# Moving expert steps out of the last attention unit, and the second half's norm into the gap behind it

## The chip, the cores and the metric

The kernel runs on one core of one Trainium2 chip. The metric is the device time of the program in microseconds, as the median of several runs. The profile is of one further execution. Its engines are TensorE (PE, with PEld for the loading of weights), VectorE (DVE), ScalarE (ACT) and GpSimd (POOL), and SyncE's queue (SP), which issues most DMAs. [...]

## The reference, cut to what matters

Tokens `x` (1024 of 128 features) pass through four layers. Each layer adds a cross-attention to a context of 6404 rows and then a mixture of experts, both on the layer-normed tokens:

```
x = x + _L1_xattn_ref(_layernorm(x), ctx, ctx, ...)
x = x + _L1_ffn_ref(_layernorm(x), ...)      # 8 experts, top 1
x = x + _L2_xattn_ref(...)                   # softmax over the heads
x = x + _L2_ffn_ref(...)                     # fake-quantised, gated
x = x + _L3_xattn_ref(...)
x = x + _L3_ffn_ref(_layernorm(x), ...)      # 8 experts, top 2
```

Attention of layers 1 and 3 has 16 heads of 8 features and a softmax over the context. An expert of layer 1 is `gelu(x w1 + b1) w2 + b2`, with `w1` of 128 x 512 and `w2` of 512 x 128; the token's best expert is added. An expert of layer 3 also adds its input, and the sum is normalised over its features, scaled by `gamma`, shifted by `beta`, and weighted by the softmax over the two best. All experts are computed for all tokens, and the weights of those not chosen are zero.

## The kernel before

The tokens are cut into two halves of 512. `attn_softmax` does attention for layers 1 and 3 in 16 units, a pair of heads and a half each; the last unit is the last pair with the second half. A unit goes over the 51 blocks of 128 keys in 26 steps. A step makes scores (L1133, `x_ps` and `y_ps`), exponentials (L1138, ACT), and the products with the values of the step before (L1023, `o_ps`). Between them, at each `M` of the step's written order, goes other work: in all units but the last the maxima of the next unit (`more_max`).

In the last unit there are no maxima left. There two generators run instead. `also` is the experts for the first half of the tokens (`ffn1` in layer 1, `ffn3` in layer 3), whose tokens are complete when the unit before is finished; `beside`, in layer 1 alone, makes the keys of layer 2 (`heads_keys`). Every step has two `M`, each of which takes one step of `beside` and, from step 9 on, one of `also`:

```
for what in order[i % 3]:
    if what == "M":
        more_max()
        next(beside, None)
        if u == UNITS - 1 and i >= 9:
            next(also, None)
```

The steps of `also` are: `normed` (layer norm on DVE with its power on POOL at L114, then, five steps on, four transposes on PE at L142 and a copy to `xnT` on DVE at L156), the router, and for each of eight experts (`expert`) twice a pair of steps. The first of a pair issues two hidden blocks (L1195 on PE, Gelu at L1196 on ACT); the second runs what waits, the second matmuls (L1184) of the part before and, after an expert's second part, the weighted add to the tokens. That is `add_weighted` in layer 1 (L624) and `add_normed` in layer 3 (L1752 to L1766: sum, statistics, a power on POOL, scaling, add). An expert's start also issues loads of its weights on SP (L1172, L1173), and in layer 3 of `gamma` and `b2` to `gb` (L1771, L1772) with two buffers, from which POOL makes `xb` (L1774).

When the unit's last values are multiplied, `finish` sets four things into the table `later`: `out_of_banks` at once (a copy by ACT and two DMAs through memory that bring the sums of the softmax to `dr`), then `inverted` (L1045, DVE, and two DMAs to `rr`), `normalized` (L1055 on PE with `rr`, L1056 on DVE), `projected` (L1062 on PE, L1066 adds to the tokens on DVE) and an empty one. Behind the last unit they are run one after the other, with five steps of `also` ahead of each, and after them whatever is left of `beside` and `also`.

PE, ACT and DVE follow the order as written in this part (`tc.manual_schedule`); POOL and SP are put in order by the framework's scheduler, from its own costs, and so is all that is outside such a part. After attention of layer 1 follow the set-up of attention of layer 2 (`attn_heads`: queries for the first half, first maxima), then the experts for the second half (`experts_apart`, which is `ffn1(1, ...)`), then the quantisation of the weights of the layer 2 network. After attention of layer 3 follow only the experts for the second half (`ffn3(1, ...)`) and the store of the output.

Of the kernel before, what the change touches and what calls it, by code (L numbers as in the profile page):

```python
# [35 lines left out]
def done(steps):  # L36

    while True:
        try:
            next(steps)  # L40
        except StopIteration as end:
            return end.value


class Net:
# [3 lines left out]
    def __init__(self, ctx, tc, a, out):  # L49
        self.tc, self.nc, self.a, self.out = tc, tc.nc, a, out  # L50
        nc = self.nc
        self.const = ctx.enter_context(tc.tile_pool(name="const", bufs=1))
        self.small = ctx.enter_context(tc.tile_pool(name="small", bufs=3))
        self.xp = ctx.enter_context(tc.tile_pool(name="xp", bufs=2))
        self.ps_h = self.ps_m = self.ps_pair = None
        self.ident = self.const.tile([P, P], F32, name="ident")
        make_identity(nc, self.ident)
        self.identb = self.const.tile([P, P], BF16, name="identb")
        nc.vector.tensor_copy(self.identb, self.ident)
        self.ones = self.const.tile([P, P], F32, name="ones")  # L60
        nc.vector.memset(self.ones, 1.0)
        self.nhalf = self.const.tile([P, NT], F32, name="nhalf")
        nc.vector.memset(self.nhalf, -0.5)
        self.cols = self.const.tile([P, a["cols"].shape[1]], F32, name="cols")
        nc.sync.dma_start(out=self.cols, in_=a["cols"])
        self.x = self.const.tile([P, NT, D], F32, name="x")
        nc.sync.dma_start(out=self.x, in_=a["x"].rearrange("(t p) d -> p t d", p=P))
# [79 lines left out]
    def normed(self, half):  # L147

        nc = self.nc
        xn = self.xp.tile([P, HT, D], F32, tag="xn", name="xn")  # L150
        xnT = self.xp.tile([P, HALF], F32, tag="xnT", name="xnT")
        self.layernorm(xn, self.tokens(half), HT)
        for _ in range(4):
            yield
        m = self.transposed(xn, HT)
        nc.vector.tensor_copy(xnT, m)  # L156
        yield
        return xn, xnT

    def tokens(self, half):  # L160
        return self.x[:, HT * half : HT * half + HT]
# [562 lines left out]
    def attn_softmax(self, ctxT, L, bo, before, last, keys_early=False):  # L724
# [18 lines left out]
        UNITS = 2 * PAIRS  # L743
# [5 lines left out]
        with ExitStack() as st:  # L749
# [256 lines left out]
            def more_max():  # L1006
                u, i = divmod(made[0], per_unit)
                if u >= UNITS:
                    return
                max_group(u, i)  # L1010
                made[0] += 1
                if i == per_unit - 1:
                    max_found(u)
                    later.setdefault(step + 2, []).append(lambda: max_to_rows(u))
# [4 lines left out]
            def values(u, i, o, pts):  # L1019
                for (c, g), pt in pts.items():  # L1020
                    h = units[u][0] + PAIRS * g
                    j = 2 * (c % 2) + g
                    nc.tensor.matmul(  # L1023
                        o[32 * j : 32 * j + 32], v[:, c, ds(VW * h, 32)], pt,
                        start=i == 0, stop=c + 2 >= NK,
                    )
# [76 lines left out]
            also = beside = iter(())  # L1103
            for u in range(UNITS):
                p = units[u][0]
                if u == UNITS - 1:
                    pairs.close()
                    self.bank_pools(tail, f"a{L}t", h=2, m=2)
                    also, beside = last(tail, kb, kS[(PAIRS - 2) % 2])
                accs[u] = None  # L1110
                pending = [(c, g) for c in range(NK) for g in range(2)]
                place = {}
                for i, cs in enumerate(pairs_of_keys):
                    for what in order[i % 3]:
                        if what == "M":
                            more_max()
                            next(beside, None)
                            if u == UNITS - 1 and i >= 9:
                                next(also, None)
                        elif what == "S":  # L1120
                            two = (len(place) % 3) == 0
                            some = [pending.pop(0) for _ in range(min(len(pending), 2 if two else 1))]
                            if not some:
                                continue
                            if two:
                                s = ps_x.tile([P, 2, HALF], F32, tag="x", name="x_ps")
                                pt = pr.tile([P, 2, HALF], F32, tag="px", name="px", bufs=3)
                            else:
                                s = ps_y.tile([P, 1, HALF], F32, tag="y", name="y_ps")
                                pt = pr.tile([P, 1, HALF], F32, tag="py", name="py", bufs=3)  # L1130
                            for k, (c, g) in enumerate(some):
                                r = slice(64 * g, 64 * g + KR)
                                nc.tensor.matmul(  # L1133
                                    s[:, k], kS[p % 2][r, ts(c, P)], qS[u % 2][r],
                                    start=True, stop=True,
                                )
                                place[c, g] = pt[:, k]
                            nc.scalar.activation(pt[:, : len(some)], s[:, : len(some)], AF.Exp)  # L1138
                        elif waiting:
                            uu, ii, pts = waiting.pop(0)  # L1140
                            if accs[uu] is None:
                                accs[uu] = ps_o.tile([P, HALF], F32, tag="o", name="o_ps")
                            values(uu, ii, accs[uu], pts)
                            if ii == STEPS - 1:
                                finish(uu, accs[uu], step)
                    waiting.append((u, i, {(c, g): place[c, g] for c in cs for g in range(2)}))
                    if made[0] < per_unit + ahead + (step + 1) * per_unit / STEPS:
                        more_max()
                    for f in later.pop(step, ()):
                        f()  # L1150
                    step += 1
# [1 line left out]
            values(uu, ii, accs[uu], pts)  # L1153
            finish(uu, accs[uu], step)
            for at in sorted(later):
                for _ in range(5):
                    next(also, None)
                for f in later[at]:
                    f()
            done(beside)  # L1160
            done(also)


# [42 lines left out]
    def ffn1(self, half, pool, w_tile, hidden_tile):  # L1206
        nc, a = self.nc, self.a
        E = 8
        wr = pool.tile([P, E], F32, name="wr")
        br = pool.tile([P, E], F32, name="br")  # L1210
        b2 = pool.tile([E, D], F32, name="b2")
        nc.sync.dma_start(out=wr, in_=a["L1_ffn_wr"])
        nc.sync.dma_start(out=br, in_=a["L1_ffn_br"].partition_broadcast(P))
        nc.sync.dma_start(out=b2, in_=a["L1_ffn_b2"])
        xn, xnT = yield from self.normed(half)
        sc = pool.tile([P, HT, E], F32, name="sc")
        nc.vector.tensor_tensor(
            sc, self.router(xnT, wr, E), br.unsqueeze(1).to_broadcast([P, HT, E]), ALU.add
        )
        cw = self.ranks_below(pool, sc, E, 1)  # L1220
        waiting = []

        def bias():
            self.add_projected(self.weights_transposed(pool, cw, E), b2, half)

        for e in range(E):
            got = yield from self.expert(1, e, xnT, w_tile, hidden_tile, waiting)
            waiting.append(lambda got=got, e=e: self.add_weighted(got["y"], half, cw, e))
            if e == 0:
                waiting.append(bias)  # L1230
        while waiting:
            waiting.pop(0)()
            yield
# [496 lines left out]
    def ffn3(self, half, pool, w_tile, hidden_tile):  # L1730
# [3 lines left out]
        beta = pool.tile([E, D], F32, name="beta")  # L1734
        nc.sync.dma_start(out=wr, in_=a["L3_ffn_router_w"])
        nc.sync.dma_start(out=beta, in_=a["L3_ffn_beta"])
        xn, xnT = yield from self.normed(half)
        lg = pool.tile([P, HT, E], F32, name="lg")
        nc.vector.tensor_copy(lg, self.router(xnT, wr, E))
        sel = self.ranks_below(pool, lg, E, 2)  # L1740
# [27 lines left out]
        for e in range(E):  # L1768
# [6 lines left out]
            got = yield from self.expert(3, e, xnT, w_tile, hidden_tile, waiting)  # L1775
# [231 lines left out]
```

## Time and profile before

| | us |
|---|---|
| median of 3 runs | 7865.02 |
| lowest and highest | 7858.43 and 7870.11 |
| the profiled execution | 7869.13 |
| its span in the profile | 7867.4 |

In the profiled execution, from the timeline:

| | layer 1 | layer 3 |
|---|---|---|
| last `o_ps` product of the unit starts | 4043.43 | 7760.00 |
| `inverted` starts on DVE (L1045) | 4052.38 | 7775.54 |
| selector matmul on PE (L1055) | 4055.93 | 7778.82 |
| projection on PE (L1062) | 4058.13 | 7781.69 |
| router of the second half's experts on PE (L575) | 4080.29 | 7789.58 |
| last second matmul of the second half's experts starts | 4139.79 | 7847.03 |

Times in the timeline are microseconds from the span's start. A row has the start, the duration, the engine, the line of the kernel, the operation with its output and inputs, and in brackets how long the engine stood idle before it and what released it. In the rows of windows, the column PEclk is the clock that was granted to PE, as a share of the full one. Granted over the whole span: 0.966.

### The profile page before, as it was taken

The numbers are of one execution on the slowest core, as the hardware profiler recorded it, in microseconds if no ns is written. First come the engines' busy times: TensorE is split into PE (matmuls) and PEld (weight loads), VectorE is DVE, ScalarE is ACT, GpSimd is POOL, SyncE is SP. The second block draws the span as 40 slices with busy tenths as digits, with TensorE's granted clock in tenths as the row PEclk, the third lists the DMA queues.
The fourth block names the chain that finished last, engine by engine and source line by source line (L and its number), as shares of the span: only waits on it lengthen the run. The fifth ranks groups of instructions, "written<-read, shape, count | busy, mean of one in ns | idle before, by whom it ended". The sixth has DMA issues, their size and how long they took to land.

```text
span 7867.4 us, 105018 instructions
## 1 busy us (share of the span) xinstructions
PE 7290.1 (93%) x41897; PEld 2775.1 (35%) x42105; DVE 5689.6 (72%) x6628; ACT 4999.0 (64%) x6063; POOL 2594.5 (33%) x1460
## 2 busy tenths in 40 slices
PE   6999999999999889999997999998899978999997
PEld 2333333333333433333343333333333333333334
DVE  6555555555553388888737999989999988888854
ACT  2444444444444457777766888877788856777765
POOL 4999989989999610000010000000000010000001
PEclk8999999999999889999998999999999988999988
DMA  1000000000000201001030000000000011101001
GB/s 30 1 2 1 2 2 1 2 2 1 1 1 1 77 24 17 15 11 20 25 122 14 14 14 13 14 11 11 12 14 13 14 51 27 19 12 20 12 6 40
DMA packets 144769, 134.94 MB, mean 17 GB/s; under 512 B 30954, under 2 KB 125478, under 8 KB 143310
## 3 DMA queue, kind: packets, MB, share of 16 engines
q1 hardware_dynamic: 134022, 105.19, 6.0%
q0 software_dynamic: 5296, 17.22, 0.7%
q8 instruction: 330, 5.41, 0.3%
q10 hardware_dynamic: 4960, 5.80, 0.2%
q14 instruction: 161, 1.32, 0.1%
HBM read 105.46 MB, written 35.85 MB: 18 GB/s over the span
## 4 chain that ended last, share of the span: by engine, by line
PE 73%; DVE 15%; ACT 5%; POOL 3%; issue 2%; DMA 1%; SPq 0%; ACTq 0%; POOLq 0%; DVEq 0%
PE o_ps L348 10%; PE x_ps L326 9%; PE s_ps L1479 8%; PE o_ps L1023 8%; DVE mx L909 8%; PE o_ps L1535 5%; PE x_ps L1133 5%; PE x_ps L1467 5%; ACT px L1138 3%; PE b_ps L281 3%; PE pair_ps L1367 3%; PE y_ps L1133 2%; PE x_ps L1463 2%; POOL acc L342 2%; PE x_ps L316 2%
## 5 line engine op out<-in xcount | busy, mean ns | idle before, releaser
L342 POOL TENSOR_TENSOR acc<-acc,pt 128x1024 f32<-128x1024 f32 x912 | 2150.0, 2357 | 116.2 <-ACT pt L331 63.0
L909 DVE TENSOR_REDUCE mx<-pair_ps 128x2 f32<-128x1024 f32 x1612 | 1811.1, 1177 | 245.9 <-PE pair_ps L905 225.9
L285 DVE TENSOR_REDUCE mx<-b_ps 128x2 f32<-128x1024 f32 x920 | 1095.0, 1190 | 1059.5 <-PE b_ps L281 1059.2
L331 ACT ACTIVATE pt<-x_ps,bias 128x1024 f32<-128x1024 f32 (+1 forms) x944 | 1003.7, 1110 | 817.8 <-PE x_ps L326 715.3
L1138 ACT ACTIVATE px<-x_ps 128x1024 f32<-128x1024 f32 x1088 | 1113.7, 1024 | 315.3 <-PE x_ps L1133 307.1
L1527 DVE TENSOR_TENSOR e<-e,inv 128x1024 f32<-128x1024 f32 (+1 forms) x816 | 993.5, 1219 | 10.7 <-DVE inv L1520 0.5
L348 PE MATMUL o_ps<-pt,v 128*64 128x512 f32 (+1 forms) x3776 | 916.0, 605 | 0.0
L1023 PE MATMUL o_ps<-px,v 128*32 128x512 f32 x4352 | 906.8, 621 | 0.0
L1023 PE MATMUL o_ps<-py,v 128*32 128x512 f32 x2176 | 899.4, 619 | 0.0
L326 PE MATMUL x_ps<-q,kT 64*128 64x512 f32 (+1 forms) x3776 | 893.5, 592 | 0.0
L1376 ACT CAST lb<-pair_ps 128x1024 bf16<-128x1024 f32 (+1 forms) x714 | 720.3, 1009 | 264.2 <-PE pair_ps L1367 239.4
L905 PE MATMUL pair_ps<-kb,qz 64*128 64x512 bf16 (+1 forms) x3224 | 823.8, 385 | 55.5 <-DVE mx L909 38.3
L1470 ACT ACTIVATE e<-x_ps 128x1024 f32<-128x1024 f32 (+1 forms) x816 | 840.5, 1030 | 24.7 <-PE x_ps L1467 22.9
L1138 ACT ACTIVATE py<-y_ps 128x512 f32<-128x512 f32 x1088 | 647.6, 595 | 325.2 <-PE y_ps L1133 321.4
L1479 PE MATMUL s_ps<-e,ident 128*128 128x512 f32 (+1 forms) x1632 | 848.4, 602 | 0.4
L1133 PE MATMUL x_ps<-qS,kS 33*128 33x512 f32 x2176 | 713.6, 533 | 126.2 <-ACT px L1138 126.1
L1133 PE MATMUL y_ps<-qS,kS 33*128 33x512 f32 x1088 | 569.2, 523 | 7.3 <-ACT py L1138 7.3
L897 POOL TENSOR_SCALAR qz<-qbf,cols 128x512 bf16<-128x512 bf16 x31 | 48.7, 1572 | 1557.0 <-PE y_ps L1133 1505.9
L1535 PE MATMUL o_ps<-e,vz 128*32 128x256 f32 (+1 forms) x6528 | 535.6, 398 | 7.6 <-DVE e L1527 7.4
L1421 POOL MEMSET kS<- 128x512 f32 x2 | 1.1, 526 | 1591.7 <-PE x_ps L1463 1591.7
L1384 DVE TENSOR_TENSOR low<-lb,low 128x1024 bf16<-128x1024 bf16 (+1 forms) x714 | 488.0, 683 | 14.3 <-ACT lb L1376 14.2
L1467 PE MATMUL x_ps<-mneg,identb 128*128 128x512 bf16 x1424 | 453.0, 388 | 40.4 <-issue 33.0
(378 smaller groups left out, 8475.6 us busy)
## 6 DMA issues: line engine op xcount, KB each, us to landing
kS<-kst SPq DMA_DIRECT2D x400, 64.0 KB
kS<-kd SPq DMA_DIRECT2D x120, 200.1 KB
w<-in_L_ffn_w SPq DMA_DIRECT2D x48, 256.0 KB
kst<-kd POOLq DMA_DIRECT2D x24, 512.0 KB, 13.4
kd<-kh SPq DMA_DIRECT2D x12, 512.0 KB
kd<-k SPq DMA_DIRECT2D x12, 512.0 KB
qS<-qd SPq DMA_DIRECT2D x256, 16.0 KB
kb<-in_L_ffn_w SPq DMA_DIRECT2D x16, 256.0 KB
```

The lines of the kernel that those rows point to most:

```text
L285: nc.vector.tensor_reduce(mxs[u][:, t, :, b], m[:, :, :n], AX.X, ALU.max)
L326: nc.tensor.matmul(s[:n, g], kT[p % 2][r, at : at + n], qs[p][r, ts(half, HALF)], start=False, stop=True,)
L331: nc.scalar.activation(pt[:n], s[:n], AF.Exp, bias=bias[:n, c : c + 1])
L342: nc.gpsimd.tensor_tensor(accs[u][:n], first[:n], pt[:n], ALU.add)
L348: nc.tensor.matmul(o[cols], v[:n, c, cols], pt[:n, g], start=c == 0, stop=c == NKT - 1)
L909: nc.vector.tensor_reduce(mxs[u][:, t, b], m[:, :, :n], AX.X, ALU.max)
L1023: nc.tensor.matmul(o[32 * j : 32 * j + 32], v[:, c, ds(VW * h, 32)], pt, start=i == 0, stop=c + 2 >= NK,)
L1133: nc.tensor.matmul(s[:, k], kS[p % 2][r, ts(c, P)], qS[u % 2][r], start=True, stop=True,)
L1138: nc.scalar.activation(pt[:, : len(some)], s[:, : len(some)], AF.Exp)
L1479: nc.tensor.matmul(firsts[i], self.ident[:n], es[i, h // 4][:n, h % 4], start=k == 0, stop=k == K - 1,)
L1527: nc.vector.tensor_tensor(e, e, r, ALU.mult)
L1535: nc.tensor.matmul(outs[half][32 * g : 32 * g + 32, cols], vz[i % 2][:n, ds(P * j + 32 * g, 32)], es[i, j][:n, g, cols], start=c == 0 and ...
```

## The change

In the last unit of layers 1 and 3, `also` is stepped at two of three steps only, the steps whose number is not a multiple of 3. Behind the unit, two of its steps go ahead of each of the four functions in `later`, instead of five. Then, with `beside` finished, the layer norm and the transposes of the second half of the tokens are issued here, with one step of `also` after each of the norm's own steps, and the result is kept in `self.ready`. The rest of `also` follows. When the experts of the second half start, they take the kept result instead of computing it (`normed_or_ready`).

```
-        self.ps_h = self.ps_m = self.ps_pair = None
+        self.ps_h = self.ps_m = self.ps_pair = self.ready = None
...
+    def normed_or_ready(self, half):
+
+        if half and self.ready:
+            got, self.ready = self.ready, None
+            return got
+        return (yield from self.normed(half))
...
-                            if u == UNITS - 1 and i >= 9:
+                            if u == UNITS - 1 and i >= 9 and i % 3:
                                 next(also, None)
...
             for at in sorted(later):
-                for _ in range(5):
+                for _ in range(2):
                     next(also, None)
                 for f in later[at]:
                     f()
             done(beside)
+
+            other = self.normed(1)
+            while True:
+                try:
+                    next(other)
+                except StopIteration as end:
+                    self.ready = end.value
+                    break
+                next(also, None)
             done(also)
...
-        xn, xnT = yield from self.normed(half)
+        xn, xnT = yield from self.normed_or_ready(half)
```

The last pair of lines stands twice, in `ffn1` and in `ffn3`.

## The prediction

> **What bounds the kernel now.** I read the page first, then the last unit of layers 1 and 3 by windows, then the chain and the timeline there. The page:
>
> ```profile
> span 7867.4 us, 105018 instructions
> PE 7290.1 (93%) x41897; PEld 2775.1 (35%) x42105; DVE 5689.6 (72%) x6628; ACT 4999.0 (64%) x6063; POOL 2594.5 (33%) x1460
> PE 73%; DVE 15%; ACT 5%; POOL 3%; issue 2%; DMA 1%; SPq 0%; ACTq 0%; POOLq 0%; DVEq 0%
> ```
>
> TensorE (PE) bounds the whole, so a gain must come from places where PE stands still. The windows of layer 3's end (start:end, length, busy PE, PEld, DVE, ACT, POOL, granted clock, DMA share, GB/s) show where:
>
> ```profile
> core 0: us, PE busy (x) PEld busy (x) DVE busy (x) ACT busy (x) POOL busy (x), PEclk, DMA share, GB/s
> 7616.00:7624.00 8.00, 7.24 (x28) 1.69 (x24) 0.00 (x0) 4.05 (x5) 0.00 (x0) 0.50 0.01 3
> 7712.00:7720.00 8.00, 8.00 (x48) 4.92 (x47) 4.66 (x17) 7.67 (x9) 1.18 (x2) 1.00 0.20 66
> 7768.00:7776.00 8.00, 0.00 (x0) 0.00 (x0) 6.38 (x21) 0.00 (x0) 1.01 (x1) 0.65 0.00 0
> 7776.00:7784.00 8.00, 4.12 (x10) 2.28 (x10) 0.88 (x2) 0.00 (x0) 0.00 (x0) 0.50 0.02 2
> 7784.00:7792.00 8.00, 3.67 (x13) 2.94 (x14) 4.17 (x19) 0.00 (x0) 3.49 (x3) 0.50 0.01 2
> ```
>
> PE is full while experts and attention share a step (second row), does nothing for 8 us after the unit (third), and limps until 7792. The timeline says why, and what a step with an expert part holds:
>
> ```profile
> 7714.22 1.98 PE L1195 MATMUL h_ps<-xnT,w 128*128 128x512 f32 x4
> 7717.97 2.05 PE L1184 MATMUL m_ps<-w,kb 128*128 128x128 f32 x16
> 7718.00 1.28 ACT L1138 ACT_TABLE_LOAD   x1
> ...
> 7769.06 0.68 DVE L1752 TENSOR_TENSOR res<-m_ps,xb 128x512 f32<-128x512 f32 x1
> 7775.54 0.16 DVE L1045 TENSOR_TENSOR dr<-dr 128x8 f32<-128x8 f32 x1
> 7778.82 2.04 PE L1055 MATMUL m_ps<-rr,selr 2*128 2x512 f32 x2 [10.94 <-DMA rr<-rd]
> 7787.55 1.25 PE L142 MATMUL m_ps<-ident,xn 128*128 128x128 f32 x4 [3.77 <-DVE xn L133]
> ```
>
> The softmax inverse (L1045) stands on DVE behind the last expert's normed add (from L1752), and PE waits 10.94 us for its round trip; then 3.77 us for the second half's norm. Layer 1 has the same tail (4.63 and 4.49 us), with cheap adds (1.13 us). Last, the chain of waits gives a step without expert work (the eight `o_ps` matmuls of each step):
>
> ```profile
> 3897.08 0.99 PE o_ps L1023 x8
> 3898.75 0.99 PE o_ps L1023 x8
> 3901.36 0.99 PE o_ps L1023 x8
> 3905.05 1.00 PE o_ps L1023 x8
> 3906.47 1.87 PE o_ps L1023 x8
> ```
>
> Four steps in 9.39 us: 2.35 us each.
>
> **The change: the loop.** `also` has 40 resumptions: 1 to 5 norm and transposes, an expert part (`h` and Gelu) at 6, 8, ... 36, and the second matmuls at the odd ones between. Before, steps 9 to 25 make 34: 15 parts in the loop, one behind it. Now eleven steps make 22: 9 parts in the loop, 7 behind it. Six parts leave the loop in each layer, with twelve ACT table loads (1.28 us each) that lie beside PE work. A step with a part takes 6.11 us in layer 3 (`h_ps` starts from 7702.32 to 7751.23, eight intervals), 6.17 in layer 1. Layer 1: 6 x 6.17 - 6 x 2.35 = 22.9 us shorter. In layer 3 the bare steps before the first part run at clock 0.50, 3.88 us each (`o_ps` from 7607.85 to 7631.13, six steps); two of the six are there: 36.7 - 2 x 3.88 - 4 x 2.35 = 19.5 us shorter.
>
> **The tail of layer 1.** From the loop's last `o_ps` (4043.96) to the projection's end (4060.21) is 16.3 us before. After, I lay PE's work end to end at 1.8 us for each `h` group or second group (4045.74 to 4047.73 in the tail of before, less its wait): four groups to 7.2; the inverse needs 0.7 (copy) + 3.8 (7610.43 to 7614.22, where nothing held it) + 0.4 + 3.1 (4052.87 to 4055.93) = 8.0, so PE waits 0.8; selector matmul 1.05; two groups; projection 1.1; six groups; transposes 0.7; four groups: end at 32.5. That is 16.2 later against 22.9 earlier: -6.7. The norm's DVE work (1.7 + 1.1 us) and POOL power (1.0) lie beside the six groups; without that cover they cost the 4.5 us they cost before.
>
> Behind it, attention of layer 2 starts. Its POOL queue held both halves' powers ahead of an all-reduce on which DVE waited 5.8 us; one power less is -1.0. The second half's expert could also start earlier than 4080.3, since its tokens are ready: between 0 and -4 (the idle PE there); I take -1. From there experts, quantisation and attention follow rigidly. Layer 1: -8.7.
>
> **The tail of layer 3.** Here an add takes some 6.1 us of DVE and POOL (7857.02 to 7863.11), and every add's `xb` needs a `gb` load which starts when the add before the last has let go:
>
> ```profile
> 7840.80 0.33 SPq L1771 DMA_DIRECT2D gb<-in_L_ffn_gamma  x1
> 7844.22 1.27 POOL L1774 TENSOR_TENSOR xb<-xn,gb 128x512 f32<-128x512 f32 x1 [5.56 <-DMA gb<-in_L_ffn_b]
> 7845.44 1.02 POOL L114 TENSOR_TENSOR rstd<-ve,nhalf 128x4 f32<-128x4 f32 x1
> ```
>
> The power stands behind that `xb` on POOL, so adds come every 7.9 us. Five now lie in the tail. In DVE's order: add 3 ends at 8.1 after the loop, the inverse behind it gives `rr` at 11.6, PE (done at 7.2) waits 4.4 us, falls to half clock and does the selector by 13.7; add 4 to 23.6; the projection's add; the norm, whose power waits for an `xb`, to 29.8; add 5 to 36.1; the `xnT` copy 36.8; add 6 to 44.0; add 7 to 50.2. The router's DVE chain follows, some 4.1 us (7791.49 to 7797.87 less its wait for ACT). Add 0 of the second half starts at 54.3; PE, at 40.4 plus 8 us for router and expert 0, is earlier. Before it was 7801.82 - 7760.53 = 41.3. So +13.0 - 19.5 = -6.5. From add 0 to the end took 61.3 before; 7 x 7.9 + 6.1 = 61.4 now: 0.
>
> SP carries all these loads. `rd` and `rr` are issued before expert 5's `gb`; were they behind it, `rr` would wait for add 3, which it does anyway. Weights are issued as their buffers come free, some 9 us ahead of use at the tail's pace against about 3 of transfer: no cost.
>
> **A rule against it.** In the trace attention-only steps ran at 0.50 with PE busy 7.24 of 8 us (7616), though the loop's first ones in layer 1 had the full clock. The Trainium skill, "TensorE: Matmul & The Clock Gate" (Part 1: The HAM clock gate), lets the clock fall after an idle window of about 3.4 us and rise after a busy one. By that rule a bare step never falls and the sum stands; by the row it may fall, at 1.53 us a step: ten bare steps that I costed at full clock would give back 15.3. I take full clock, because single bare steps stand between full ones and layer 1 held it for some 10 us without maxima.
>
> **Sum.** -8.7 - 6.5 = -15.2, against the profiled execution's 7869.1: 7853.9. It stood 4.1 above the median 7865.0, so 7850.
>
> **Rivals.**
> - Larger gain: the scheduler puts the first expert of layer 1's second half into idle PE (-4 instead of -1), and layer 3's router chain into DVE's waits for POOL (-4.1): about 7842, and 7835 if some adds come closer as well. For it: PE's idle time at 4067 to 4080. Against: one PE queue, and loads that land late there.
> - The bare steps fall to half clock: 15.3 given back, 7865.
> - Layer 3 gives nothing: the `xnT` copy stands behind add 5 and the add chain carries its delay to the end, only layer 1's -6 or so stays: 7859. For it: DVE's strict order at 7769 to 7775.
> - Slower: the clock. If a bare step drops the clock and the next part's dense work (4 us) starts at half, each such step costs 1.53 + 4 = 5.5 us. Three of ten eat the gain and six pass 0.2%; seven give 38.5 - 15.2 = +23, or 7888. For it: the 0.50 at 7616 and the slow return after 7776. Against: parts follow within 2.35 us.
> - The change not doing what it says (the second norm recomputed) I exclude: `ready` is taken for half 1 only.
>
> **How the numbers follow.** The sum as worked, 7840 to 7858: 0.50, half of it on either side of 7849; the larger gain 0.13; half clock 0.13; layer 3 nothing 0.10; slower 0.14. About 0.2% (15.7 us) is what a measurement of this kernel can tell from no change. Faster: 0.13 + 0.25 = 0.38; within: 0.25 + 0.23 = 0.48; slower 0.14. The range runs from the larger gain's end, with run scatter of 4 us, to the mild end of the clock cases: 7832 to 7872.
>
> **What would show it.** Six fewer pairs of table loads within each last unit; steps of 2.4 us between those of 6.1; PE waiting under 1 us for `rr` in layer 1 and about 4 in layer 3; no norm between projection and router; add 0 of the last phase some 6 us earlier. Wrong would be: a clock of 0.50 in bare steps after the first part, PE waiting on `xnT` for more than 4 us, or attention of layer 2 starting no earlier.

## The result: 0.27% slower, and the profile after

| | before | after |
|---|---|---|
| median of 7 runs, us | 7871.40 | 7894.72 |
| lowest and highest | 7858.43 and 7873.95 | 7879.55 and 7912.32 |
| the profiled execution | 7869.13 | 7912.32 |
| its span | 7867.4 | 7910.6 |

The ratio is 1.0027, with a 95% interval of 1.0018 to 1.0036; the medians lie 23 us apart. Four more executions put the median of before at 7871.40, where three had given 7865.02. The prediction said 7850, a gain, and a loss came. The profiled execution of the changed kernel happened to be the slowest of its seven, so its 43 us are not all due to the change. The table of stages below takes that apart.

The page of the changed kernel (span, busy time by engine, share of the chain by engine):

```profile
span 7910.6 us, 105181 instructions
PE 7368.3 (93%) x42105; PEld 2797.6 (35%) x42105; DVE 5690.4 (72%) x6628; ACT 4973.3 (63%) x6039; POOL 2596.5 (33%) x1460
PE 72%; DVE 15%; ACT 5%; POOL 4%; issue 2%; DMA 2%; SPq 0%; ACTq 0%; POOLq 0%; DVEq 0%
```

ACT has 24 instructions fewer, the twelve table loads in each layer that the prediction took away. PE has the same work, yet 78 us more of busy time. Part of that is records that the trace of before lacks (x41897 against x42105, less than 0.5%). The rest fits a lower clock: 0.959 was granted over the whole span, against 0.966 before. The next view shows where.

Windows of layer 3's end (start:end, length, busy PE, PEld, DVE, ACT, POOL, granted clock, DMA share, GB/s). In the changed kernel the lines of before from L160 on to those of attention (L575, L1023, L1055, L1138) stand 7 further down, and those of the experts (L1184, L1195, L1196) 16 further:

```profile
core 0: us, PE busy (x) PEld busy (x) DVE busy (x) ACT busy (x) POOL busy (x), PEclk, DMA share, GB/s
7644.00:7652.00 8.00, 7.25 (x30) 1.74 (x26) 0.00 (x0) 4.05 (x5) 0.00 (x0) 0.50 0.02 4
...
7756.00:7764.00 8.00, 8.00 (x30) 4.76 (x29) 0.00 (x0) 2.22 (x4) 1.27 (x1) 0.50 0.05 12
...
7788.00:7796.00 8.00, 4.34 (x22) 2.56 (x21) 4.56 (x18) 2.75 (x4) 1.02 (x1) 0.93 0.34 83
7796.00:7804.00 8.00, 6.04 (x19) 4.41 (x20) 0.94 (x2) 0.00 (x0) 1.26 (x1) 0.50 0.00 1
...
7812.00:7820.00 8.00, 8.00 (x49) 5.90 (x48) 4.22 (x18) 2.75 (x4) 5.58 (x5) 1.00 0.12 36
```

The first row is the limp ahead of the first part, as before. The third and the last are of the tail, which did what was hoped for: PE is half busy or full where it did nothing for 8 us (7768 to 7776 of before). The second row is new. In the middle of the expert steps, where before had clock 1.00 in each window from 7704 to 7768, PE is full, but at half clock. The timeline of layer 1 shows how it comes to that (start, duration, engine, line, operation, idle time before and its releaser):

```profile
4018.03 1.98 PE L1211 MATMUL h_ps<-xnT,kb 128*128 128x512 f32 x4
...
4019.24 1.28 ACT L1212 ACT_TABLE_LOAD   x1
4019.94 0.50 PE L1140 MATMUL y_ps<-qS,kS 33*128 33x512 f32 x1
...
4020.53 1.27 ACT L1212 ACTIVATE kb<-h_ps,cols 128x512 f32<-128x512 f32 x2
...
4021.82 1.28 ACT L1145 ACT_TABLE_LOAD   x1
4023.11 0.60 ACT L1145 ACTIVATE py<-y_ps 128x512 f32<-128x512 f32 x1
...
4023.76 0.79 PE L1140 MATMUL y_ps<-qS,kS 33*128 33x512 f32 x1 [1.90 <-ACT py L1145]
...
4027.99 3.78 PE L1200 MATMUL m_ps<-kb 128*128 128x128 f32 x16
...
4032.42 2.46 PE L1211 MATMUL h_ps<-xnT,w 128*128 128x512 f32 x4
...
4036.24 2.05 PE L1200 MATMUL m_ps<-kb 128*128 128x128 f32 x16
...
4044.39 0.50 PE L1140 MATMUL y_ps<-qS,kS 33*128 33x512 f32 x1 [1.90 <-ACT py L1145]
```

A part's Gelu holds ACT for 1.28 + 1.27 + 1.28 us, and the exponential of the score tile that PE wrote from 4019.94 on starts at 4023.11. Where the next step holds a part as well, PE has second matmuls to do meanwhile. A bare step (one without a part) has none: PE waits 1.90 us for the tile to come free. The matmul that ends the wait takes 0.79 us, not 0.50: the clock is down, and it stays down for the bare step and for the second matmuls behind it (`m_ps` 3.78 in place of 2.05 us). Windows of 3.41 us show how long:

```profile
4019.77:4023.18 3.41, 2.09 (x12) 0.53 (x11) 0.00 (x0) 3.37 (x5) 0.00 (x0) 1.00 0.34 99
4023.18:4026.59 3.41, 2.71 (x11) 0.77 (x11) 0.00 (x0) 3.03 (x4) 0.00 (x0) 0.50 0.00 0
4026.59:4030.01 3.42, 3.42 (x14) 2.31 (x11) 0.00 (x0) 0.61 (x2) 0.00 (x0) 0.50 0.00 0
4030.01:4033.42 3.41, 3.41 (x12) 2.25 (x11) 0.00 (x0) 0.83 (x1) 0.00 (x0) 0.50 0.00 0
4033.42:4036.83 3.41, 3.41 (x18) 1.31 (x17) 0.00 (x0) 3.36 (x5) 0.00 (x0) 1.00 0.00 0
```

The clock fell before the wait was over and came back at 4033.42, some 10.2 us later, though PE was full from 4026.59 on. The last line of the timeline is the same wait in the next turn: the matmul behind it takes 0.50 us, and the clock falls only at 4047, inside the part behind. The chain of waits gives the price; from one turn of three steps (bare, part, part) to the next:

```profile
4014.26 1.00 PE o_ps L1030 x8
...
4025.47 1.86 PE o_ps L1030 x8
...
4034.88 1.00 PE o_ps L1030 x8
```

4014.26 to 4034.88 are 20.6 us, where the prediction had 2 x 6.17 + 2.35 = 14.7, and where three steps with a part took 18.5 before. Two parts with a bare step between them are slower than three parts.

The tails, on PE:

```profile
4063.10 1.09 PE L1062 MATMUL m_ps<-rr,selr 2*128 2x512 f32 x2 [1.55 <-DMA rr<-rd]
...
7797.96 2.04 PE L1062 MATMUL m_ps<-rr,selr 2*128 2x512 f32 x2 [5.62 <-DMA rr<-rd]
...
7823.63 3.84 PE L1200 MATMUL m_ps<-w,kb 128*128 128x128 f32 x32 [2.08 <-DVE xnT L156]
...
7840.15 1.01 PE L611 MATMUL m_ps<-ident,cwr 128*8 128x128 f32 x4 [3.06 <-DVE cwr L603]
```

The waits for `rr` fell from 4.63 and 10.94 to 1.55 and 5.62 us, and the second half's transposes no longer stand bare behind the projection.

### The profile page after: what moved, and what is told of

It is laid out like the page before. It is cut to its first block, busy times and chain, and to the rows that moved or that the text cites. A ratio compares the mean times of both kernels' runs of the same rounds, so it can differ in the third digit from the quotient of the medians.

```text
span 7910.6 us, 105181 instructions
## 1 busy us (share of the span) xinstructions
PE 7368.3 (93%) x42105; PEld 2797.6 (35%) x42105; DVE 5690.4 (72%) x6628; ACT 4973.3 (63%) x6039; POOL 2596.5 (33%) x1460
## 4 chain that ended last, share of the span: by engine, by line
PE 72%; DVE 15%; ACT 5%; POOL 4%; issue 2%; DMA 2%; SPq 0%; ACTq 0%; POOLq 0%; DVEq 0%
PE o_ps L355 10%; PE x_ps L333 9%; PE s_ps L1495 8%; PE o_ps L1030 8%; DVE mx L916 7%; PE o_ps L1551 5%; PE x_ps L1483 5%; PE x_ps L1140 5%; ACT px L1145 3%; POOL acc L349 3%; PE pair_ps L1383 3%; PE b_ps L288 3%; PE y_ps L1140 2%; PE x_ps L1479 2%; PE pair_ps L912 2%
## 5 line engine op out<-in xcount | busy, mean ns | idle before, releaser
L1483 PE MATMUL x_ps<-mneg,identb 128*128 128x512 bf16 x1632 | 502.5, 390 | 7.4 <-DVE mneg L1405 7.4
```

## The experiments

One table for all of them, worked out from the timeline of each kernel's profiled execution. "Loop" runs from the start of the last `mx` reduction on DVE to the start of the unit's last group of `o_ps`. "Behind" runs from there to the first `s_ps` matmul of layer 2's attention in layer 1, and to the end of the span in layer 3. "Rest" is what is left of the span, work that no kernel here touches.

| kernel | ratio to before (95%) | loop 1 | behind 1 | loop 3 | behind 3 | rest |
|---|---|---|---|---|---|---|
| before | | 145.9 | 134.0 | 165.7 | 108.7 | 7313 |
| after | 1.0027 (1.0018 to 1.0036) | 142.9 | 140.9 | 162.5 | 127.4 | 7337 |
| a_loop_only | 1.0043 (1.0029 to 1.0056) | 148.3 | 149.7 | 152.9 | 132.6 | 7329 |
| b_norm_only | 0.9994 (0.9983 to 1.0004) | 141.1 | 135.8 | 162.9 | 111.2 | 7314 |
| c_bare_last | 0.9998 (0.9989 to 1.0008) | 131.1 | 140.7 | 149.7 | 124.1 | 7321 |
| d_bare_first | 0.9993 (0.9985 to 1.0001) | 128.9 | 139.8 | 152.2 | 123.4 | 7323 |
| e_lin_before | 0.9988 (0.9980 to 0.9996) | 139.6 | 135.2 | 151.4 | 110.6 | 7331 |
| f_lin_after | 0.9980 (0.9971 to 0.9990) | 129.5 | 139.3 | 136.9 | 124.3 | 7311 |
| g_one_only | 0.9994 (0.9985 to 1.0002) | 128.9 | 139.4 | 166.2 | 110.3 | 7321 |
| h_filled | 1.0002 (0.9994 to 1.0010) | 130.8 | 139.3 | 142.9 | 124.0 | 7328 |
| i_warm3 | 0.9990 (0.9984 to 0.9997) | 142.7 | 134.9 | 152.8 | 110.7 | 7326 |
| j_both | 0.9983 (0.9972 to 0.9994) | 129.3 | 139.2 | 151.6 | 109.7 | 7336 |

The rest wanders between 7311 and 7337 us with no order in it, so the stages say more than a span. They wander too: the loop of layer 1 that before, b and i have in common took 145.9, 141.1 and 142.7, and that of layer 3 in before, b and g 165.7, 162.9 and 166.2. A difference of under 5 us in one stage means nothing here. The identical loops of the changed kernel and of a_loop_only in layer 3 (162.5 and 152.9) differ by more: after the last maxima began, the clock stayed at 1.00 for 28 us in a_loop_only and for 10 in the changed kernel. The stages behind the loops wander less: those of layer 1 lie between 134.0 and 135.8 in the four kernels with the old loop there (before, b, e, i).

The stages of the changed kernel sum to 19.4 us more than those of before, near the 23.3 us between the medians.

The theory after the comparison (theory 1): a bare step behind a part costs 5.9 us more than I gave it, by the wait for ACT and the clock that falls in it. The rivals: the longer tails (rival 2), or the early norm (rival 3), cost the time.

**One half of the change alone.** First the thinned loop without the early norm, then the early norm without the thinned loop.

```
a_loop_only, against the changed kernel:
-            other = self.normed(1)
-            while True:
...
b_norm_only, against the changed kernel:
-                            if u == UNITS - 1 and i >= 9 and i % 3:
+                            if u == UNITS - 1 and i >= 9:
...
-                for _ in range(2):
+                for _ in range(5):
```

> The thinned loop and the two steps of also ahead of each later function are kept; the second half's norm and transposes are made where they were before, at the start of the second half's experts. Theory 1 (a step without an expert part, standing between two with one, finds ACT still busy with Gelu and two table loads; PE waits some 2 us, its clock falls, and the next part runs at half clock; such a step costs about 8.3 us in place of 2.35): three steps of the last unit take about 20.6 us as in the changed kernel, and the whole is 20 to 40 us slower than before. Rival 2 (the longer tails cost the time, not the loop): also slower, by about 20 us, but with the loop some 20 us shorter than before. Rival 3 (the early norm costs the time, through its place in DVE's and POOL's queues): as fast as before or up to 15 us faster.

> Only the early norm and transposes are kept; the loop takes an expert part in every step from 9 on and five steps of also go ahead of each later function, as before. Theory 1 (steps without a part in the loop): no such steps after the first part, so the loop is as before; the norm's waits go, in layer 1 with an earlier start of the second half's experts: 5 to 12 us faster than before. Rival 2 (the longer tails): about the same as before, since the tails are the old ones. Rival 3 (the early norm): slower than before by 10 to 20 us.

The loop alone loses no less than the whole change: 7906.70 us, with 7875.53 for before (the intervals of 1.0043 and 1.0027 overlap). Its turn of three steps in layer 1 is 20.7 us (`o_ps` at 4017.27 and 4037.97). So rival 3 is out: the early norm is no cost, and in this arrangement it is worth 8.8 us behind the loop of layer 1 (149.7 to 140.9) and 5.2 us in layer 3, in one execution of each. The norm alone gave 7866.80, with an interval that holds no change; I had expected 5 to 12 us of gain. Its stages behind the loops are not shorter than before (135.8 against 134.0, 111.2 against 108.7). By the code, the one part left behind the loop is used up before the norm, so nothing is left to put beside it.

**The same number of parts, other places.** In both kernels the nine parts are one after the other.

```
c_bare_last:
-                            if u == UNITS - 1 and i >= 9 and i % 3:
+                            if u == UNITS - 1 and 9 <= i < 20:
d_bare_first:
-                            if u == UNITS - 1 and i >= 9 and i % 3:
+                            if u == UNITS - 1 and i >= 15:
```

> As the changed kernel, with as many expert parts in the loop (9), but in eleven steps one after the other (9 to 19), so that the six steps without a part stand together at the loop's end. Theory 1: one return from a part to bare steps in each layer in place of five; four times 5.9 us less in each layer, 47 us, of which up to 15 us can be lost again if the bare steps run at half clock (3.88 in place of 2.35 us): 10 us faster than before, between 27 faster and 5 slower. Rival 2 (tails): the tails are those of the changed kernel, so 20 us slower than before, as it is. Rival 3 (early norm): the same, 20 us slower.

> As the changed kernel, with as many parts in the loop, but begun later (step 15) and then in every step, so that no step without a part follows one with a part. Theory 1: the loop is about 18 to 23 us shorter than before in layer 1 and 13 us in layer 3 (its bare steps run at half clock, 3.88 us, as they do before the first part now); with the tails of the changed kernel 7 us faster than before, between 15 faster and 2 slower. Rivals 2 and 3: the tails and the norm are those of the changed kernel, so about 20 us slower than before.

They took 7873.52 and 7866.29 us against 7875.53 of before: the loss is gone with nothing changed but the place of the bare steps. Rival 2 is out, since the tails are those of the changed kernel. Which of the two places is better is not shown: their intervals overlap. The loops are 15 to 17 us shorter than before in layer 1 and 13 to 16 in layer 3. Of the 10 us that I expected from c_bare_last, 2 came. Windows of its last steps in layer 3 show why:

```profile
core 0: us, PE busy (x) PEld busy (x) DVE busy (x) ACT busy (x) POOL busy (x), PEclk, DMA share, GB/s
7713.00:7721.00 8.00, 7.66 (x40) 3.60 (x42) 4.05 (x15) 7.49 (x9) 1.02 (x1) 1.00 0.28 81
7721.00:7729.00 8.00, 4.96 (x29) 1.41 (x25) 0.00 (x0) 6.83 (x10) 1.28 (x1) 0.88 0.00 0
7729.00:7737.00 8.00, 7.74 (x31) 1.69 (x23) 0.00 (x0) 4.13 (x6) 0.00 (x0) 0.50 0.01 3
```

The first bare step lets the clock fall, and the others stay at half: 3.86 us a step on average (`o_ps` from 7720.71 to 7739.99, five steps).

**Without the table loads.** Is it Gelu's two table loads that make PE wait, or has a bare step too little work for the clock in any case?

```
-                    hid[:, j], h, AF.Gelu, bias=self.col(f"L{L}_b1", 4 * e + k)
+                    hid[:, j], h, AF.Identity, bias=self.col(f"L{L}_b1", 4 * e + k)
```

> The kernel before with the experts' Gelu replaced by the identity (with the same bias), so that the last unit's steps need no change of ACT's table; the experts' values are not the reference's. It is the base for the next run. All theories: PE is full in the steps with a part, so the loop stays within 5 us of before in each layer; 0 to 10 us faster than before.

> The changed kernel with the same replacement of Gelu by the identity. Theory 1a (the two table loads around Gelu put ACT behind, and that makes PE wait in a step without a part, after which the clock falls): without them three steps take about 15 us in place of 20.6, and the kernel is 10 to 15 us faster than the kernel before with the same replacement. Theory 1b (a step without a part has too little work for PE's clock, whatever ACT does): three steps still take 18 us or more, and the kernel is 10 to 25 us slower than the kernel before with the replacement.

With the identity the change turns from a loss of 23 into a gain of 9 us: 7866.05 for the kernel before so altered, 7856.92 for the changed one (their intervals against before overlap). That is theory 1a, a little below its 10 to 15. The chain of f_lin_after has the rest:

```profile
3999.73 0.99 PE o_ps L1030 x8
...
4001.27 1.03 ACT px L1145
...
4002.85 0.99 PE o_ps L1030 x8
...
4004.28 3.56 PE m_ps L1200 x16
...
4011.59 1.98 PE m_ps L1200 x16
...
4016.34 1.00 PE o_ps L1030 x8
```

Three steps take 16.6 us, not 15. The bare step alone is 3.1 us, since it is always one of the kind with three groups of scores (`"SMSMSP"`), and here the clock still fell for a moment (3.56). So 1b holds a small part, 1.9 us over the 14.7 of the prediction. The base moved more than I expected in layer 3's loop (151.4 against 165.7).

**Something for PE to do in the wait.** The changed kernel, with two matmuls in the bare step that nobody reads.

```
                                next(also, None)
+                            elif u == UNITS - 1 and i >= 15 and place_free != i:
+                                place_free, warm = i, self.m_tile()
+                                for _ in range(2):
+                                    nc.tensor.matmul(
+                                        warm, self.ident, wo[:, :4].rearrange("p a d -> p (a d)"),
+                                        start=True, stop=True,
+                                    )
```

> The changed kernel with two more matmuls of 128x512 that nobody reads (about 2 us of PE) at the first M of each of the steps 15, 18, 21 and 24 of the last unit, where PE waits 1.9 us for the exponentials. Theory 1, as far as it rests on the clock: PE's wait is filled, the clock stays at 1.00, the next part takes 4 us and not 7.7; three steps take about 17 us in place of 20.6, and with eight such places the kernel is 20 to 30 us faster than the changed kernel, so within 10 us of before. Rival (PE is held by ACT's work and the clock doesn't matter): the added matmuls change nothing or cost up to 16 us more, 25 to 40 us slower than before.

The timeline of h_filled, at the place of the timeline above (its `m_ps` of L1208 are the second matmuls):

```profile
4021.86 1.27 ACT L1220 ACTIVATE kb<-h_ps,cols 128x512 f32<-128x512 f32 x2
...
4023.11 1.98 PE L1131 MATMUL m_ps<-wo,ident 128*128 128x512 f32 x4
...
4025.09 0.50 PE L1148 MATMUL y_ps<-qS,kS 33*128 33x512 f32 x1
...
4027.85 2.05 PE L1208 MATMUL m_ps<-w,kb 128*128 128x128 f32 x16
```

The useless matmuls fill the wait to its end, the next score takes 0.50 us and the second matmuls 2.05. Three steps take 16.6 us (`o_ps` at 4009.79 and 4026.43), 4.0 less than in the changed kernel. Sixteen matmuls in all brought the kernel from 1.0027 to 1.0002 of before. This separates the two halves of the cost: ACT's backlog is the same (that score starts 3.4 us into the step in both kernels), only PE's clock is kept, and most of the loss is gone. The stages of this execution would give 17 us less than before; the medians show 1. Some 10 us of that may be chance, an estimate from the 162.5 and 152.9 above: its layer 3 loop of 142.9 had the full clock for 28 us after the last maxima began, as a_loop_only had.

**Towards a better kernel.** In layer 1 the later start, in layer 3 the loop of before; then PE's clock in layer 3 ahead of the first part; then both.

```
g_one_only, against the changed kernel:
-                            if u == UNITS - 1 and i >= 9 and i % 3:
+                            if u == UNITS - 1 and i >= (15 if L == 1 else 9):
i_warm3, against the kernel before (j_both has it on top of g_one_only):
+                            if L == 3 and u == UNITS - 1 and i < 12 and filled != i:
+                                filled, warm = i, self.m_tile()
+                                nc.tensor.matmul(
+                                    warm[:, :256], self.ident, wo[:, :2].rearrange("p a d -> p (a d)"),
+                                    start=True, stop=True,
+                                )
```

> The later start of the expert parts (step 15, then every step) in layer 1 alone, where it shortened the way from the last maxima to the next attention by 8 to 11 us; in layer 3 a part in every step from 9 on as before. The early norm and two steps of also ahead of each later function in both layers; in layer 3 fewer adds then stand ahead of the softmax inverse on DVE. Theory 1 (bare steps between parts cost, parts moved into PE's idle time of layer 1's tail gain): layer 1 8 to 11 us shorter, layer 3 2 to 7 us: 10 to 18 us faster than before. Rival (layer 1's gain is only scatter of the clock): within 5 us of before.

> The kernel before with one more matmul of 128x256 that nobody reads (about 0.5 us of PE at full clock) at the first M of each step below 12 of layer 3's last unit, where the steps without an expert part ran at clock 0.50 and took 3.88 us. If PE's share of busy time is what holds the clock: it stays near 1.00, the steps take 2.4 to 2.9 us, twelve of them save 12 to 18 us: 10 to 18 us faster than before. Rival (the clock falls there whatever PE is given, since ACT sets the pace): the added matmuls cost up to 1 us each at half clock: 0 to 12 us slower.

> The expert parts of layer 1 from step 15 on, those of layer 3 from step 9 on in every step, the early norm and two steps of also ahead of each later function in both, and the added matmuls in layer 3's steps below 12 as in the run beside it. If the gains add up: 5 to 10 us of the later start in layer 1 and 10 to 18 us of the clock in layer 3: 15 to 25 us faster than before. If the clock isn't held: 5 us faster to 7 slower.

g_one_only took 7867.04 against 7873.61 us, and its interval holds no change: layer 1 gave 11.6 us in its stages (8 to 11 expected), layer 3 nothing. Fewer adds stood ahead of the inverse, so the selector matmul came 13.7 us behind the loop in place of 20.1, but add 0 of the second half stayed at 43.0 (43.1 before). PE's wait had only moved: 4.49 us for `rr` and 8.57 for the norm, where before had 10.94 and 3.77.

i_warm3 is faster than before by 0.1%, 7866.55 against 7874.74 us. Windows of its bare steps in layer 3:

```profile
core 0: us, PE busy (x) PEld busy (x) DVE busy (x) ACT busy (x) POOL busy (x), PEclk, DMA share, GB/s
...
7617.00:7625.00 8.00, 7.88 (x40) 2.78 (x42) 0.37 (x2) 6.44 (x10) 0.00 (x0) 1.00 0.03 3
7625.00:7633.00 8.00, 7.88 (x45) 2.64 (x37) 0.00 (x0) 6.11 (x8) 0.00 (x0) 1.00 0.01 2
...
7641.00:7649.00 8.00, 7.78 (x41) 3.00 (x37) 1.91 (x7) 5.61 (x9) 3.56 (x3) 1.00 0.00 0
```

A matmul of 0.70 us in each step holds the clock where before had 0.50. The loop is 12.9 us shorter, within the 10 to 18 expected; the median shows 8. A loop as short came up without the added matmuls too (152.9 in a_loop_only, where the clock happened to hold), so the median is the better measure. j_both adds layer 1's later start: 7859.54 against 7874.74 us, ratio 0.9983 (0.9972 to 0.9994), the 15 us of the expectation's lower end. Its interval lies below those of both kernels of this case, but not below that of i_warm3.

## Why the prediction was wrong, point by point

- **The price of a bare step: the step that failed.** "2.35 us each" came from steps behind other bare steps, where ACT had no Gelu to finish. It was also a mean over steps of 1.4 to 3.7 us, while each bare step of the change is of the kind with three score groups. Behind a part a bare step measured 5.03 us (`o_ps` 4020.37 to 4025.40) and the part after it 9.41 (to 4034.81). Against 2.35 and 6.17 that is 2.7 + 3.2 = 5.9 us. There were eight such steps; after one (it ended at 7739.31) no drop followed, and after the last in each layer half of one (6.7 us for a last part, 5.1 before): eight times 2.7 and six times 3.2 make 41, an estimate. The loops were to be 22.9 and 19.5 us shorter and were 3.0 and 3.2, so 36 us were missing; the 5 between are within the scatter of the loops.
- **The rule against it.** The prediction weighed the row at 0.50 against the Trainium skill, "TensorE: Matmul & The Clock Gate" (Part 1: The HAM clock gate), whose clock falls after an idle window of some 3.4 us, and took full clock. The runs side with the row: five of the eight bare steps lost the clock in a wait, three of these of 1.89 to 1.91 us, and layer 3's loop lost it at 7631 with no PE wait above 0.95 us since the last maxima. But the length of a wait doesn't decide alone. Two waits of 1.90 us left the next matmul at full speed (4044.39), and so did this one of 3.21 in f_lin_after, where the windows from 7768 to 7784 show clock 1.00:

```profile
7773.69 0.60 PE L611 MATMUL m_ps<-ident,cwr 128*8 128x128 f32 x4 [3.21 <-DVE cwr L603]
```

The same page's section on a second failure mode (psum-queue depth-cycling) tells of another kernel, in bf16, where frequent short waits between groups of matmuls let the clock swing. It is nearer to this case, in which PE waits for a score tile to come free and, with that wait filled in h_filled, keeps its clock. What exactly makes the clock fall stays open.

- **The rival "Slower: the clock"** was the right one, and close in size: 5.5 us guessed for a place, 5.9 measured; 7888 for seven places, 7894.7 measured. I gave it 0.14. The closeness is in part luck: 1.53 + 4 was guessed where 2.7 + 3.2 came, and the errors of the two tails nearly cancel. Its mechanism lacked the cause of the wait: "parts follow within 2.35 us" spoke against it, and ACT's 3.8 us of loads and Gelu were costed at nothing, the loads as lying "beside PE work", without asking what covers them once the next step has no second matmuls.
- **The tail of layer 1** was costed well up to its end: from the loop's last `o_ps` to its end 17.9 us longer (36.0 against 18.1) for 16.2 predicted. From there to the next attention it was 11.0 us shorter (104.9 against 115.9) for 2 predicted: the second half's matmuls start as soon as the first half's end (`h_ps` at 4088.27), as the rival "Larger gain" had it.
- **The tail of layer 3:** add 0 came 13.6 us later behind the loop (56.7 against 43.1), for +13.0. From add 0 to the end 0 was predicted and 5.1 measured, with a PE wait of 3.06 for `cwr` in which the clock falls again (0.71 from 7836 to 7844). In c, d and h, with the same tail, waits of 1.4 to 1.5 us and no drop, it was 1.1 to 1.3 us.
- **The sum:** against what was predicted, the loops lack 36 us, layer 1 behind its loop is 7 us better and layer 3 is 6 us worse. Together that is the 35 us between a gain of 15.2 and the loss of 19.4 in the stages.
- **The signs named:** the table loads and the place of the norm came as said; the waits for `rr` were 1.55 and 5.62 for "under 1" and "about 4". The steps of 2.4 us between those of 6.1 did not come, and add 0 came no earlier (7839.9, 7801.8 before). Of the signs of being wrong, the clock of 0.50 is there, and attention of layer 2 started 3.9 us later after the last maxima (283.8 against 279.9).

## What to carry to other kernels

Work that is taken out of a step leaves the others' latencies uncovered: before costing the emptied step by a row, ask which engine's backlog the removed matmuls used to hide, and take the row from a step that follows the same neighbour. Here a PE wait of 2 us was mostly paid twice, by itself and by the half clock of the dense work behind it; bare steps did better together than between dense ones. Where PE is only just not full, a small matmul that nobody reads can be cheaper than the clock that is lost without it.

## What the runs showed of the hardware

- In five of the eight bare steps behind a part PE's clock fell to 0.50 in a wait of 1.89 to 3.49 us, and each time it came back only some 10.2 us later (4023.18 to 4033.42). After two waits of 1.90 us it fell later, inside the next part; after one of 0.78 us (7735.57) it did not fall.
- Once down, it stayed at 0.50 with PE busy 7.25 of 8 us (7644). At full clock the same steps showed PE busy some 6.7 of 8 us in a_loop_only (7627 to 7651). With 7.78 to 7.88 of 8 it stayed at 1.00 in i_warm3.
- When it falls is not the same in each execution: in layer 3's bare steps it held for 10 us after the last maxima began in the changed kernel and for 28 us in a_loop_only, which has the same loop. In all ten kernels without the added matmuls there it was at 0.50 within 30 us; in the two with them it held until the first part. Stages of equal code differ by up to 10 us.
- Sixteen matmuls without use made a kernel some 20 us faster.
